# Time attention with one mixed block of scores a step, layer-norm roots by ScalarE, and both additions of weights on POOL

## The chip, the cores and the metric

One core of one Trainium2 chip. The metric is the device time of the whole kernel in microseconds (us). Executions repeat within 0.3% for all but one of the kernels below; that one has a section of its own. Kernels sent together ran on the same chip beside runs of the kernel before.

## The reference

The input x has 2 x 256 x 128 x 128 float32 elements (batch, time T, bands FB, channels C). One layer, three residual parts:

```python
xt = _ln(x, ln_t_w, ln_t_b).transpose(0, 2, 1, 3)
x = x + _mha(xt, t_wi, t_bi, t_wo, t_bo, 4, causal_mask(256)).transpose(0, 2, 1, 3)   # over time
xf = _ln(x, ln_f_w, ln_f_b)
x = x + _mha(xf, f_wi, f_bi, f_wo, f_bo, 4, band_mask(128, 16))                       # over bands
xn = _ln(x, ln_n_w, ln_n_b)
x = x + (gelu(xn @ w1.T + b1) @ w2.T + b2)                                            # feed-forward
# _ln: (x - mean) * rsqrt(var + 1e-5);  _mha: 4 heads of 32 channels, softmax
```

All bias vectors of the inputs are zero. This matters for one experiment.

## The kernel before

Everything stays in float32. Work goes in groups of 512 rows (four tiles of 128). For time attention a group is two sequences of 256 steps, so the causal scores of a sequence have three blocks of 128x128: first keys with both halves of the queries (256 columns), second keys with the second half (128 columns). There are 128 such groups, one in each step of a software pipeline. All instructions of an engine run in program order. The code is shortened:

```python
def root(self):                                    # layer norm, on POOL: (var + EPS) ** -0.5
    gpsimd.tensor_scalar(self.rstd, self.mv[:, :, 1], EPS, None, ALU.add)
    gpsimd.tensor_tensor(self.rstd, self.rstd, path.k.mhalf, ALU.pow)
def normalize(self):                               # VectorE, four tiles: xh
    for i in range(NT):
        vector.tensor_scalar(self.xh[:, i, :], self.src()[:, i, :], self.mv[:, i, 0:1], self.rstd[:, i : i + 1],
                             ALU.subtract, ALU.mult)
def bias(self):                                    # POOL: residual + folded bias row -> res
    self.path.gpsimd.tensor_tensor(self.dst(), self.src(), orow_of_this_attention, ALU.add)
def divide(self):                                  # VectorE: softmax division with one Newton step
    vector.tensor_tensor(by_rows(t), by_tile(self.rp), by_tile(self.r0), ALU.mult)
    vector.tensor_tensor(by_rows(u), by_tile(self.op), by_tile(self.r0), ALU.mult)
    vector.scalar_tensor_tensor(self.oT, t, 2.0, u, ALU.subtract, ALU.mult)
# ... (cut)
class OverTime(Attention):
    def scores(self, s):                           # sequence s: four heads = four row tiles of 32
        for h in range(H):
            path.tensor.matmul(self.sp[h][:, 0:2*P], self.kT[r, a:a+P], self.qT[r, a:a+2*P], ...)
        for h in range(H):
            path.tensor.matmul(self.sp[h][:, 2*P:3*P], self.kT[r, a+P:a+2*P], self.qT[r, a+P:a+2*P], ...)
    # exp on ScalarE (128x384 a head), two causal masks of 128x512 a sequence on POOL,
    # one addition of weights on POOL (sequence 0), one on VectorE (sequence 1)
# ... (cut)
def bank(self, shape, name):                       # PSUM: eight buffers of one tag
    return self.ps.tile(shape, F32, name=name, tag="ps")
```

On TensorE the projections, sums and outputs work on four column tiles (128x32 weights). The scores work on four row tiles (32x128 weights), in two blocks a step, one for each sequence.

## Time and profile before

| | before |
|---|---|
| median | 2786.06 us (2785.55 to 2786.35, 3 runs) |
| 128 time groups | 46 to about 1040 us, 7.63 us a step on TensorE |
| bands and feed-forward | the remaining 1745 us, not meant to change |
| engines, 200 to 962 us, of 762 | PE 762, VectorE 671, ScalarE 614, POOL 702 |

PE is TensorE's matmuls, PEld its weight loads, DVE is VectorE, ACT is ScalarE. A timeline line gives the start, the duration, engine, operation, output and inputs, shapes and how many in a row. In brackets stands the idle time ahead of it and what ended that time. The tiles: qp, kp and vp are the projections, sp the scores, rp the sums of the softmax, op the weighted values, yp the output product; r, t, u and oT belong to the division; stats and mv are the statistics of the layer norm, rstd its root, xh the normalized rows, z their transpose; res is the residual, first with the bias row (POOL), then with yp added (VectorE). For "steps" I take the differences between the starts of rp, once a step on TensorE. The lines themselves are in the prediction.

### The profile page before, as it was taken

What the parts mean: (1) busy time and instruction counts of PE and PEld (TensorE: products, weight loads), DVE (VectorE), ACT (ScalarE), POOL (GpSimd) and SP (SyncE); (2) the same over time, 40 slices, a digit from 0 to 9 for tenths busy, and PEclk for the clock granted to TensorE, in tenths of its full rate; (3) what the DMA queues carried; (4) which work ended last, traced back from release to release, by engine and by line L of the source; (5) the groups of instructions that cost most, each with busy time, mean ns of one, the idle gap of its engine ahead of it and who ended that gap; (6) DMA issues with size and microseconds to landing.
All of it is one profiled execution on the core that took longest, in us unless ns stands there. A gap on an engine that the chain in (4) does not pass through costs nothing.

```text
span 2785.2 us, 103938 instructions
## 1 busy us (share of the span) xinstructions
PE 2730.3 (98%) x42534; PEld 1867.5 (67%) x42534; DVE 2221.5 (80%) x6446; ACT 1800.0 (65%) x3328; POOL 2079.3 (75%) x2569
## 2 busy tenths in 40 slices
PE   4999999999999989999999999999999999999998
PEld 3666666666666657776777777777777767767776
DVE  5888888888888898778678687687786786876874
ACT  2888888878888866646556556456466465574563
POOL 3899999999999997667676676676676666766762
PEclk9999999999999999999999999999999999999999
DMA  5555555555555554544544544535545445444333
GB/s 121 135 147 137 137 141 143 146 132 146 139 142 135 146 134 117 129 117 102 140 105 111 132 106 123 130 100 127 127 99 137 104 108 130 113 117 114 91 92 85
DMA packets 471301, 343.70 MB, mean 123 GB/s; under 512 B 43296, under 2 KB 405152, under 8 KB 470816
## 3 DMA queue, kind: packets, MB, share of 16 engines
q1 hardware_dynamic: 469568, 335.92, 47.5%
q8 instruction: 337, 5.52, 0.9%
q14 instruction: 148, 1.21, 0.2%
q10 hardware_dynamic: 1248, 1.05, 0.1%
HBM read 169.03 MB, written 167.77 MB: 121 GB/s over the span
## 4 chain that ended last, share of the span: by engine, by line
PE 93%; DVE 3%; DMA 2%; POOL 1%; issue 0%; SPq 0%; ACT 0%; DVEq 0%; POOLq 0%
PE zp L848 17%; PE hp L848 16%; PE sp L848 12%; PE op L848 10%; PE qp L848 8%; PE rp L848 8%; PE vp L848 8%; PE yp L848 7%; PE kp L848 7%; POOL pt L848 1%; DMA x<-in_x 1%; DVE xh L848 1%; DMA xnT<-turned 1%; DVE oT L848 0%; POOL rstd L848 0%; DVE stats L848 0%
## 5 line engine op out<-in xcount | busy, mean ns | idle before, releaser
L848 ACT ACTIVATE hT<-hp,b 128x512 f32<-128x512 f32 x512 | 348.7, 687 | 546.0 <-PE hp L848 536.1
L848 POOL TENSOR_SCALAR_AFFINE_SELECT pf<-pf 128x512 f32<-128x512 f32 x768 | 541.5, 720 | 173.5 <-ACT pf L848 147.1
L848 PEld LDWEIGHTS zp<-w2T_sb,hT 128*128 128x128 f32 x4096 | 476.4, 192 | 56.1 <-issue 54.0
L848 DVE TENSOR_SCALAR xh<-x,mv,rstd 128x128 f32<-128x128 f32 x1536 | 509.2, 392 | 0.4 <-POOL rstd L848 0.4
L848 PE MATMUL zp<-w2T_sb,hT 128*128 128x128 f32 x4096 | 479.8, 275 | 0.1
L848 PE MATMUL hp<-xnT,w1f 128*128 128x512 f32 x1024 | 469.2, 596 | 3.6 <-DMA xnT<-turned 3.4
L848 POOL TENSOR_TENSOR rstd<-rstd,mhalf 128x4 f32<-128x4 f32 x384 | 441.3, 1149 | 32.0
L848 ACT ACTIVATE pt<-sp 128x384 f32<-128x384 f32 x1024 | 419.5, 497 | 58.8 <-PE sp L848 58.8
L848 PE MATMUL sp<-qT,kT 32*128 32x128 f32 (+1 forms) x8192 | 389.5, 315 | 0.8 <-ACT kT L848 0.8
L848 POOL TENSOR_SCALAR_AFFINE_SELECT pt<-pt 128x512 f32<-128x512 f32 x512 | 322.7, 651 | 79.0 <-ACT pt L848 79.0
L848 PEld LDWEIGHTS sp<-qT,kT 32*128 32x128 f32 x8192 | 310.9, 185 | 79.7 <-issue 31.1
L848 POOL TENSOR_SCALAR rstd<-mv 128x4 f32<-128x4 f32 x384 | 89.2, 232 | 365.5 <-DVE mv L848 365.1
L848 DVE BATCH_NORM_STATS2 stats<-x 128x6 f32<-128x128 f32 x1536 | 329.0, 274 | 7.6 <-DMA x<-in_x 7.6
L848 ACT ACTIVATE pf<-sp 128x512 f32<-128x512 f32 x512 | 264.3, 603 | 58.8 <-PE sp L848 52.4
L848 PEld LDWEIGHTS hp<-xnT,w1f 128*128 128x128 f32 x1024 | 182.2, 190 | 178.9 <-issue 109.6
L848 PE MATMUL qp<-xnT,wf 128*32 128x512 f32 (+1 forms) x1856 | 273.1, 600 | 26.2 <-DVE xh L848 26.2
L848 PEld LDWEIGHTS yp<-wn,oT 128*32 128x32 f32 (+1 forms) x7808 | 240.8, 111 | 84.0 <-issue 63.2
L848 PEld LDWEIGHTS vp<-wf,xnT 128*32 128x32 f32 (+1 forms) x7424 | 241.1, 113 | 70.4 <-issue 60.2
L848 DVE STREAM_TRANSPOSE z<-xh 128x512 f32<-128x512 f32 x384 | 273.2, 711 | 18.9 <-DMA turned<-z 5.8
L848 PE MATMUL yp<-wn,oT 128*32 128x128 f32 (+1 forms) x7808 | 277.9, 273 | 0.3 <-DVE t L848 0.3
L848 DVE TENSOR_TENSOR res<-zp,res 128x512 f32<-128x512 f32 x128 | 87.6, 685 | 234.8 <-PE zp L848 234.7
L848 PE MATMUL vp<-wf,xnT 128*32 128x128 f32 (+1 forms) x7424 | 273.5, 273 | 0.5 <-DVE t L848 0.5
(90 smaller groups left out, 4072.8 us busy)
## 6 DMA issues: line engine op xcount, KB each, us to landing
turned<-z SPq DMA_DIRECT2D x1536, 64.0 KB, 2.2
xnT<-turned SPq DMA_DIRECT2D x384, 256.0 KB, 2.8
x<-in_x SPq DMA_DIRECT2D x128, 256.0 KB, 4.8
x<-res SPq DMA_DIRECT2D x256, 128.0 KB, 3.4
x<-x SPq DMA_DIRECT2D x128, 256.0 KB, 4.1
out<-res SPq DMA_DIRECT2D x256, 128.0 KB, 2.4
w1T_sb<-in_w1T ACTq DMA_DIRECT2D x1, 256.0 KB, 3.9
w2T_sb<-in_w2T ACTq DMA_DIRECT2D x1, 256.0 KB, 4.2
```

The lines of the kernel that those rows point to most:

```text
L848: return self.tc.keep_in_program_order(emit(*args, **kwargs))
```

## The change

Each switch to row tiles costs TensorE time (about 0.36 us in this trace, worked out in the prediction), so the change makes one block of scores a step out of two. The short second-key scores of group n and the long first-key scores of group n+1 are issued together, with the heads interleaved so that the four row tiles have equal work. That moves the pipeline of the time groups one step earlier. To make room on POOL for both additions, the roots go to ScalarE as Exp(-0.5 Ln(var + eps)), followed by one Newton step of three tiny VectorE instructions. Each PSUM bank becomes a tag of its own, so that banks can be placed by hand. The diff, shortened:

```diff
+    def root_by_scalar(self):
+        var = self.mv[:, :, 1]
+        path.scalar.activation(ln, var, AF.Ln, bias=path.eps)
+        path.scalar.activation(y, ln, AF.Exp, scale=-0.5)
+        vector.scalar_tensor_tensor(t, var, EPS, y, ALU.add, ALU.mult)
+        vector.scalar_tensor_tensor(t, t, -0.5, y, ALU.mult, ALU.mult)
+        vector.scalar_tensor_tensor(self.rstd, t, 1.5, y, ALU.add, ALU.mult)
 ... (cut)
-    def last_sum(self):
-        self.add(self.path.vector, 1)
+    def mask(self, blk):                  # one mask of 128x1024 for two of 128x512
+    def add(self, s):
+        self.path.gpsimd.tensor_tensor(self.p1[:, s, :, 1], self.p1[:, s, :, 0], self.p0[:, s, :, P : 2 * P], ALU.add)
+def time_scores(old, new):
+    for h, second, s in (
+        (0, 1, 0), (1, 0, 0), (2, 0, 0), (3, 1, 0), (0, 1, 1), (3, 1, 1), (0, 0, 0), (3, 0, 0),
+        (1, 0, 1), (2, 0, 1), (0, 0, 1), (3, 0, 1), (1, 1, 0), (2, 1, 0), (1, 1, 1), (2, 1, 1),
+    ):
+        if second and old is not None:
+            old.second_scores(h, s)
+        if not second and new is not None:
+            new.first_scores(h, s)
 ... (cut: order of the step)
+            if old is not None or new is not None:
+                time_scores(old, new)
+                Attention.place = dict(rp=b["b0"], op=b["b3"], yp=b["a1"], qp=b["a2"], kp=b["b1"], vp=b["b2"])
+                old.mask_second()
+                old.add(0)
+                new.mask_first()
+                old.add(1)
-            do_at(n + 4, OverTime, "root")
+            do_at(n + 5, OverTime, "root_by_scalar")
 ... (cut)
-        return self.ps.tile(shape, F32, name=name, tag="ps")
+            i, self.next_bank = self.next_bank, (self.next_bank + 1) % 8
+        return self.ps.tile(shape, F32, name=name, tag=f"ps{i}")
```

More of the change, by code (lines that the diff above doesn't have):

```diff
@@ L468, in root @@
         gpsimd.tensor_tensor(self.rstd, self.rstd, path.k.mhalf, ALU.pow)
+    def root_by_scalar(self):
+        path, vector = self.path, self.path.vector
+        var = self.mv[:, :, 1]
+        ln = path.small.tile([P, NT], F32, name="lnv")
+        path.scalar.activation(ln, var, AF.Ln, bias=path.eps)
+        y = path.small.tile([P, NT], F32, name="y")
+        path.scalar.activation(y, ln, AF.Exp, scale=-0.5)
+        t = path.small.tile([P, NT], F32, name="vy")
+        vector.scalar_tensor_tensor(t, var, EPS, y, ALU.add, ALU.mult)
+        vector.scalar_tensor_tensor(t, t, -0.5, y, ALU.mult, ALU.mult)
+        self.rstd = path.small.tile([P, NT], F32, name="rstd", bufs=16)
+        vector.scalar_tensor_tensor(self.rstd, t, 1.5, y, ALU.add, ALU.mult)
     def normalize(self):
@@ L512, in second_mask @@
         pass
-    def last_sum(self):
-        pass
     def queries_keys(self):
@@ L549 @@
     which = None
+    place = {}
     def bias(self):
@@ L558, in queries_keys @@
         wf = path.k.wf[self.which]
-        self.qp = path.bank([P, NT * P], "qp")
+        self.qp = path.bank([P, NT * P], "qp", self.place.get("qp"))
         product(path, self.qp, wf[:, 0:P], self.xnT)
-        self.kp = path.bank([P, NT * P], "kp")
+        self.kp = path.bank([P, NT * P], "kp", self.place.get("kp"))
         product(path, self.kp, wf[:, P : 2 * P], self.xnT)
@@ L577, in values @@
         wv = path.k.wf[self.which][:, 2 * P : 3 * P]
-        self.vp = path.bank([P, NT, P], "vp")
+        self.vp = path.bank([P, NT, P], "vp", self.place.get("vp"))
         for i in range(NT):
@@ L583, in take_values @@
         path = self.path
-        self.v = path.work.tile([P, NT, P], F32, name="v")
+        self.v = path.work.tile([P, NT, P], F32, name="v", bufs=4)
         path.scalar.copy(self.v, self.vp)
@@ L617, in output @@
         path = self.path
-        self.yp = path.bank([P, NT, P], "yp")
+        self.yp = path.bank([P, NT, P], "yp", self.place.get("yp"))
         for i in range(NT):
@@ L646, with first_tiles @@
     which = 0
-    W = 3 * P
-    def scores(self, s):
+    early, late = (1, 2), (0, 3)
+    def first_tiles(self):
         path = self.path
-        W, a = self.W, 2 * s * P
-        self.sp = [path.bank([P, W], "sp") for h in range(H)]
-        for h in range(H):
-            r = rows_of(h)
-            path.tensor.matmul(
-                self.sp[h][:, 0 : 2 * P], self.kT[r, a : a + P], self.qT[r, a : a + 2 * P], start=True, stop=True
-            )
-        for h in range(H):
-            r = rows_of(h)
-            path.tensor.matmul(
-                self.sp[h][:, 2 * P : W], self.kT[r, a + P : a + 2 * P], self.qT[r, a + P : a + 2 * P],
-                start=True, stop=True,
-            )
@@ L665, in weights @@
-    def weights(self, s):
-        path = self.path
-        for h in range(H):
-            path.scalar.activation(self.p[:, s, h, 0 : self.W], self.sp[h], AF.Exp)
-    def mask(self, s):
-        path = self.path
-        for n in (2, 0):
-            blk = self.block(s, n)
-            path.gpsimd.affine_select(
-                out=blk, in_=blk, compare_op=ALU.is_ge, fill=path.zero, base=0,
-                pattern=[[0, H], [1, P]], channel_multiplier=-1,
-            )
-    def block(self, s, n):
-        return self.p[:, s, :, n * P : (n + 1) * P]
@@ L682, in add @@
-    def add(self, engine, s):
-        engine.tensor_tensor(self.block(s, 3), self.block(s, 1), self.block(s, 2), ALU.add)
-    def first_half(self):
-        self.p = self.path.work.tile([P, 2, H, self.W + P], F32, name="pt", tag="p", bufs=2)
-        self.scores(0)
-    def first_function(self):
-        self.weights(0)
-    def first_mask(self):
-        self.mask(0)
-        self.add(self.path.gpsimd, 0)
-    def second_half(self):
-        self.scores(1)
-    def second_function(self):
-        self.weights(1)
@@ L702, in second_mask @@
-    def second_mask(self):
-        self.mask(1)
-    def last_sum(self):
-        self.add(self.path.vector, 1)
-    def weigh_one(self, op, s):
-        path, p, v, W = self.path, self.p, self.v, self.W
-        for h in range(H):
-            r = rows_of(h)
-            path.tensor.matmul(op[r, s, :], v[:, 2 * s, r], p[:, s, h, 0 : 2 * P], start=True, stop=False)
-        for h in range(H):
-            r = rows_of(h)
-            path.tensor.matmul(
-                op[r, s, P : 2 * P], v[:, 2 * s + 1, r], p[:, s, h, 2 * P : W], start=False, stop=True
-            )
@@ L719, in weigh @@
-    def weigh(self):
-        path = self.path
-        op = path.bank([P, 2, 2 * P], "op")
-        rp = path.bank([P, 2, 2 * P], "rp")
-        self.weigh_one(op, 0)
-        sums = self.p.rearrange("p s h (n q) -> p s h n q", q=P)[:, :, :, 0:4:3, :]
-        for h in range(H):
-            path.tensor.matmul(rp[rows_of(h), :, :], path.k.ones[:, 0:D], sums[:, :, h], start=True, stop=True)
-        self.weigh_one(op, 1)
-        self.op = op.rearrange("p s q -> p (s q)")
-        self.rp = rp.rearrange("p s q -> p (s q)")
+        self.p0 = path.work.tile([P, 2, H, 2 * P], F32, name="p0", tag="p", bufs=3)
@@ new lines, in first_tiles, with second_tiles, first_scores @@
+        self.s0 = {h: path.bank([P, 2, 2 * P], "sp", path.banks[f"a{h}"]) for h in range(H)}
+    def second_tiles(self):
+        path = self.path
+        self.p1 = path.work.tile([P, 2, H, 2, P], F32, name="p1", tag="h", bufs=2)
+        self.s1 = {h: path.bank([P, 2, P], "sp", path.banks[f"b{h}"]) for h in range(H)}
+    def first_scores(self, h, s):
+        r, a = rows_of(h), 2 * s * P
+        self.path.tensor.matmul(
+            self.s0[h][:, s], self.kT[r, a : a + P], self.qT[r, a : a + 2 * P], start=True, stop=True
+        )
@@ new lines, in second_scores, with first_weights, second_weights @@
+    def second_scores(self, h, s):
+        r, a = rows_of(h), (2 * s + 1) * P
+        self.path.tensor.matmul(
+            self.s1[h][:, s], self.kT[r, a : a + P], self.qT[r, a : a + P], start=True, stop=True
+        )
+    def first_weights(self, heads):
+        for h in heads:
+            self.path.scalar.activation(self.p0[:, :, h], self.s0[h], AF.Exp)
+    def second_weights(self, heads):
+        for h in heads:
+            self.path.scalar.activation(self.p1[:, :, h, 0], self.s1[h], AF.Exp)
@@ new lines, in mask, with mask_first, mask_second @@
+    def mask(self, blk):
+        path = self.path
+        path.gpsimd.affine_select(
+            out=blk, in_=blk, compare_op=ALU.is_ge, fill=path.zero, base=0,
+            pattern=[[0, 2], [0, H], [1, P]], channel_multiplier=-1,
+        )
+    def mask_first(self):
+        self.mask(self.p0[:, :, :, 0:P])
+    def mask_second(self):
+        self.mask(self.p1[:, :, :, 0])
+    def add(self, s):
+        self.path.gpsimd.tensor_tensor(self.p1[:, s, :, 1], self.p1[:, s, :, 0], self.p0[:, s, :, P : 2 * P], ALU.add)
@@ new lines, in weigh @@
+    def weigh(self):
+        path, v = self.path, self.v
+        rp = path.bank([P, 2, 2, P], "rp", self.place.get("rp"))
+        for n in range(2):
+            for h in range(H):
+                w = self.p1[:, :, h, 1] if n else self.p0[:, :, h, 0:P]
+                path.tensor.matmul(rp[rows_of(h), :, n], path.k.ones[:, 0:D], w, start=True, stop=True)
+        op = path.bank([P, 2, 2 * P], "op", self.place.get("op"))
+        for s in range(2):
+            for h in range(H):
+                r = rows_of(h)
+                path.tensor.matmul(op[r, s, :], v[:, 2 * s, r], self.p0[:, s, h], start=True, stop=False)
+            for h in range(H):
+                r = rows_of(h)
+                path.tensor.matmul(
+                    op[r, s, P : 2 * P], v[:, 2 * s + 1, r], self.p1[:, s, h, 0], start=False, stop=True
+                )
+        self.op = op.rearrange("p s q -> p (s q)")
+        self.rp = rp.rearrange("p s n q -> p (s n q)")
@@ new lines, in time_scores @@
+def time_scores(old, new):
+    if new is not None:
+        new.first_tiles()
+    if old is not None:
+        old.second_tiles()
+    for h, second, s in (
[6 more added lines that the diff above has]
+            new.first_scores(h, s)
@@ L767, in first_half @@
     def first_half(self):
-        self.p = self.path.work.tile([P, H, NT, P], F32, name="pf", tag="p", bufs=2)
+        self.p = self.path.work.tile([P, H, NT, P], F32, name="pf", tag="p", bufs=3)
         self.scores(range(H))
@@ L810, in first_half @@
         self.hp = {}
-        self.hT = self.path.work.tile([P, self.path.k.NI, NT * P], F32, name="hT")
+        self.hT = self.path.work.tile([P, self.path.k.NI, NT * P], F32, name="hT", tag="h", bufs=2)
         self.hidden((0, 1))
@@ L858, in __init__ @@
         self.small = ctx.enter_context(tc.tile_pool(name="small", bufs=6))
-        self.ps = ctx.enter_context(tc.tile_pool(name="ps", bufs=8, space=PSUM))
+        self.ps = ctx.enter_context(tc.tile_pool(name="ps", bufs=1, space=PSUM))
+        self.next_bank = 0
+        self.banks = dict(zip(("a1", "a2", "b0", "b3", "a0", "a3", "b1", "b2"), range(8)))
         self.tensor, self.vector = InOrder(tc, tc.nc.tensor), InOrder(tc, tc.nc.vector)
@@ L864, in __init__ @@
         once = ctx.enter_context(tc.tile_pool(name="once", bufs=1))
+        self.eps = once.tile([P, 1], F32, name="eps")
+        tc.nc.vector.memset(self.eps, EPS)
         self.band = once.tile([P, P], F32, name="band")
@@ L872, in __init__, with bank @@
             )
-    def bank(self, shape, name):
-        return self.ps.tile(shape, F32, name=name, tag="ps")
+    def bank(self, shape, name, i=None):
+        if i is None:
+            i, self.next_bank = self.next_bank, (self.next_bank + 1) % 8
+        return self.ps.tile(shape, F32, name=name, tag=f"ps{i}")
     @staticmethod
@@ L978, in run @@
             turn = feeds[2] and bands[1]
+            old, new = (groups[i] if at(i, OverTime) else None for i in (n, n + 1))
             self.by_columns = at(n - 1, Attention)
             do(n + 11, "load")
-            do_at(n + 4, OverTime, "statistics")
             if bands[2] and feeds[1]:
@@ L985, in run @@
             do(n, "first_half", "first_function", "first_mask")
+            if old is not None or new is not None:
+                time_scores(old, new)
+                b = self.banks
+                Attention.place = dict(rp=b["b0"], op=b["b3"], yp=b["a1"], qp=b["a2"], kp=b["b1"], vp=b["b2"])
+            else:
+                Attention.place = {}
+            if old is not None:
+                old.second_weights(old.late)
+            if new is not None:
+                new.first_weights(new.early)
+            if old is not None:
+                old.second_weights(old.early)
+                old.mask_second()
+                old.add(0)
             if turn:
                 do(n, "second_half", "second_function")
-            do_at(n + 2, Attention, "fetch")
+            do_at(n + 3, OverTime, "fetch")
+            do_at(n + 2, OverBands, "fetch")
             do_at(n + 1, FeedForward, "fetch")
             do_at(n + 2, FeedForward, "normalize", "turn")
-            do_at(n + 3, Attention, "normalize", "turn")
-            do_at(n + 4, OverTime, "root")
+            do_at(n + 3, OverBands, "normalize", "turn")
+            do_at(n + 4, OverTime, "normalize", "turn")
+            do_at(n + 5, OverTime, "statistics")
             if bands[2]:
@@ L996, in run @@
             do(n - 1, "invert_exactly" if turn else "invert")
-            if bands[2] or turn:
+            if new is not None:
+                new.first_weights(new.late)
+                new.mask_first()
+            if old is not None:
+                old.add(1)
+            if bands[2] or turn or old is not None:
                 do(n - 2, "output", "finish")
@@ L1008, in run @@
                 if not turn:
-                    do_at(n + A, OverBands, "statistics", "root")
-            do(n + 1, "queries_keys", "take_query", "take_key")
-            if not bands[2] and not turn:
-                do(n - 2, "output", "finish")
-            do(n + 1, "values", "take_values")
-            do(n, "last_sum")
+                    do_at(n + A, OverBands, "statistics")
+                    if not at(n, OverTime):
+                        do_at(n + A, OverBands, "root")
+            do_at(n + 2, OverTime, "queries_keys", "take_query", "take_key")
+            do_at(n + 1, OverBands, "queries_keys", "take_query", "take_key")
+            do_at(n + 5, OverTime, "root_by_scalar")
+            if at(n - 1, OverTime):
+                do_at(n + A - 1, OverBands, "root_by_scalar")
+            if not bands[2] and not turn and old is None:
+                do(n - 2, "output", "finish")
+            do_at(n + 2, OverTime, "values", "take_values")
+            do_at(n + 1, OverBands, "values", "take_values")
+            if old is not None or new is not None:
+                b = self.banks
+                self.banks = dict(
+                    a1=b["a1"], a2=b["a2"], b0=b["a0"], b3=b["a3"], a0=b["b0"], a3=b["b1"], b1=b["b3"], b2=b["b2"]
+                )
 def bounded_path(tc, k, x, out):
```

## The prediction

> **What bounds the kernel now.** I read the page's busy shares first, then the busy time by stretch, then the timeline of one step on TensorE, and last the groups and the timeline of VectorE and POOL for what they wait on each other.
>
> ```profile
> PE 2730.3 (98%) x42534; PEld 1867.5 (67%) x42534; DVE 2221.5 (80%) x6446; ACT 1800.0 (65%) x3328; POOL 2079.3 (75%) x2569
> ```
>
> PE covers the whole span. The 128 time-attention groups run from 46 us to about 1040 us, one group a step; only they change. The stretches (PE, PEld, DVE, ACT, POOL busy) show two regimes there:
>
> ```profile
> 200.00:962.00 762.00, 762.00 (x15190) 480.33 (x15190) 671.09 (x1801) 613.56 (x1300) 702.09 (x800) 1.00 0.55 141
> 962.00:1034.00 72.00, 64.41 (x1268) 39.96 (x1264) 70.80 (x178) 50.77 (x108) 70.76 (x80) 1.00 0.48 123
> ```
>
> For 762 us PE never idles. In the last 72 us (the last eight steps, which also normalize the first band groups) DVE and POOL are 98% busy and PE idles 7.6 us. One step on PE:
>
> ```profile
> 507.23 0.94 PE L848 MATMUL sp<-qT,kT 32*128 32x256 f32 x16
> 508.10 1.06 PE L848 MATMUL qp<-xnT,wf 128*32 128x512 f32 x8
> 508.98 1.04 PE L848 MATMUL kp<-xnT,wf 128*32 128x512 f32 x8
> 509.84 1.06 PE L848 MATMUL yp<-wn,oT 128*32 128x128 f32 x32
> 510.71 1.06 PE L848 MATMUL vp<-wf,xnT 128*32 128x128 f32 x32
> 511.70 0.94 PE L848 MATMUL sp<-qT,kT 32*128 32x256 f32 x16
> 512.56 0.86 PE L848 MATMUL op<-pt,v 128*32 128x256 f32 x16
> 513.24 1.04 PE L848 MATMUL rp<-pt,ones 128*32 128x512 f32 x8
> 514.09 0.83 PE L848 MATMUL op<-pt,v 128*32 128x256 f32 x16
> 514.86 0.94 PE L848 MATMUL sp<-qT,kT 32*128 32x256 f32 x16
> ```
>
> Read the differences of starts, since the ends are modelled: the step is 514.86 - 507.23 = 7.63 us. Products of 512 columns on four column tiles take 0.86 (kp, yp, rp). A block of scores streams 384 columns a row tile, so 384/512 x 0.86 = 0.645 us, but lasts 0.87: 0.22 over. The product ahead of a block is longer too: vp 0.99 against yp's 0.87 (0.12), the second op 0.77 against 0.645. Each block of row tiles so costs about 0.22 + 0.12 + 0.02 = **0.355 us** beside its streaming, twice a step.
>
> **What the Trainium skill says.** "TensorEngine Tiling (Array Packing)", Key Properties: a change of tiling mode drains TensorE. The trace agrees; above is its price here. "TensorE: Matmul & The Clock Gate", LDWEIGHTS: a load costs by its columns, whatever its rows; this agrees with 185 ns for 32x128 weights against 110 for 128x32, and with the first pass of a block being late. "GPSIMD Engine Reference", Key points: it shares SBUF interfaces with VectorE and contends with instructions in a 2-port mode or with two SBUF inputs. The trace agrees, strongly:
>
> ```profile
> 501.89 0.69 DVE L848 SCALAR_TENSOR_TENSOR oT<-t,u 128x512 f32<-128x512 f32 x1
> 994.29 1.28 POOL L848 TENSOR_TENSOR pt<-pt 128x512 f32<-128x512 f32 x1
> 994.36 1.77 DVE L848 SCALAR_TENSOR_TENSOR oT<-t,u 128x512 f32<-128x512 f32 x1
> 506.21 1.39 DVE L848 TENSOR_SCALAR xh<-x,mv,rstd 128x128 f32<-128x128 f32 x4
> 998.50 1.71 POOL L848 TENSOR_TENSOR res<-x,orow 128x512 f32<-128x512 f32 x1
> 999.00 3.05 DVE L848 TENSOR_SCALAR xh<-x,mv,rstd 128x128 f32<-128x128 f32 x4
> ```
>
> oT alone is 0.69 us; begun inside POOL's addition it ends 0.55 us after the addition does. The four xh take 1.1 to 1.4 us, or 3.05 when POOL has work one after another: each then waits out one whole POOL instruction. Masks (0.63) hold DVE as additions do; the tiny pow (1.04) does not: xh runs beside it at 0.34. Stats, the transpose and what reads PSUM (t, u, res) are never held. "ScalarE: Activation LUTs", Table sets: ln and exp share a set, so roots on ACT should need no table load; the Ln and Exp of the reciprocal already alternate here without one.
>
> **The change, part by part.**
> *PE.* The first-key-block scores of group n+1 and the second-key-block scores of group n are issued as one block: still 768 columns a row tile, 1.29 us. The heads' order gives row tiles 0 and 3 the short ones first and 1 and 2 the long ones, so all finish together if tiles run independently; today's records show h0 to h3 starting 7 ns apart, so I assume it. One of two blocks' 0.355 us goes: step 7.63 - 0.355 = **7.27 us**, the floor. Over 120 full steps: -42.6 us.
> *ACT.* Eight exps of 384 become four of 512 and four of 256: starts lie 0.37 apart now, 0.48 for 512 and, by the slope, 0.265 for 256: 2.98 us both ways. Added: Ln and Exp of 128x4, about 0.45 us. From 613.56/100 = 6.14 to 6.6 us a step. Fits. kT ends about 0.85 us after kp does (as in the bands) and vp lasts 0.98, so the scores should not wait for it.
> *POOL.* Removed: the root, 0.23 + 1.15 a step. Two masks of 1024 for four of 512: 2 x 1.08 (estimate from 292 ns at 128 and 630 at 512) for 2.52. Added: one addition, 1.29. Left: 2.16 + 3 x 1.26 = 5.95 of work, against 7.03 busy with waits.
> *DVE.* Minus the addition (1.06), plus three 128x4 instructions (0.15 to 0.2 each, like small ones here): 6.71 - 1.06 + 0.5 = 6.15.
> Each engine fits 7.27 alone. **Together DVE and POOL hardly do.** All of POOL's 5.95 us now hold the interface; the pow, which didn't, is gone. And DVE's contending instructions now stand in a row: oT, three small root instructions (two SBUF inputs), four xh.
> By hand, from the start of the scores: all second exps end 2.9, so POOL runs first mask 2.96 to 4.03, addition to 5.25, second mask to 6.3, addition to 7.57, bias after it. DVE's res waits for yp until 4.85, then t, u; oT is ready at 6.8, waits for the second addition and ends 8.1; bias then holds until 9.25, the root's three wait for it, and xh starts at 9.75, that is 2.5 in the next step. Two xh pass, then the mask comes at 2.96, and the last two wait until 4.05 and 5.3. res comes at 7.1 to 7.8, while PE's next block wants its bank (yp's) at 7.27. PE waits about 0.6, and 0.3 more for op's bank behind u. That delay lets xh pass freely in the following step, and the next good one fails again: 7.27 and about 8.15 in turn, mean 7.7. Were xh 0.35 us earlier, all would fit and 7.27 would hold. My timings are no better than that, so I take the mean of 7.27 and 7.7, **7.5**, as expected: 120 x (7.63 - 7.5) = -16 us.
> *Last eight steps.* Now 8.15, 8.47, 9.71, 9.70, 9.55, 8.32, 8.33, 8.32 between sums on PE. Without the roots POOL has 5.95 + 1.27 (band bias) = 7.2, DVE 6.15 + 1.5 (band statistics and roots), plus waits for each other: some 8.2 each, -5 us.
> *Fill.* One more step of software pipeline: 0 to +2 us. Bands and feed-forward keep their order on the engines; their buffers stay sufficient.
> Sum: 2786 - 16 - 5 = 2765.
>
> **Rivals.** (1) *The floor holds*: 7.27 everywhere; -42.6, about -8 at the tail: 2735. For it: PE is at 100% with other engines under 92%, and the author placed every bank so that it is freed in time. Against it: the interface. (2) *The interface becomes the bound*: 7.7 or a bit more: 2790. For it: the hand timetable; the last eight steps of before, where PE idles with DVE and POOL saturated. (3) *The mixed block doesn't run level* (a row tile waits in order behind a longer one): up to 0.21 us, one 128-column pair, of the gain gone, 25 us: about 2760 without contention. Nothing in the trace has mixed lengths. (4) *kT or v late on ACT* behind the small roots: under 0.1 us a step.
>
> **Range and chances.** Over 2% faster needs below 2730, beyond even rival 1: 5%. Over 2% slower needs a step above 8.1 us: 4%. Predicted 2764, from 2735 (rival 1) to 2803 (rival 2 with a longer tail or a ragged block).
>
> **What would show it.** Steps on PE between starts of rp: 7.27 flat (rival 1), or alternating 7.27 and 8+ (rival 2). The scores' block should last 1.29 + 0.22 with one gap of 0.12 ahead; more is rival 3. Under rival 2 the waits show scores on PE released by DVE (res or u), and means of xh and oT above 392 and 839 ns. I am wrong if small root instructions are not held by POOL, for then xh is early enough; or if the new block loses more than it saves.

## The result and the profile after

The changed kernel takes **2835.03 us** (median of 4 runs, 2831.26 to 2838.56) beside 2785.81 us of the kernel before in the same rounds. The ratio is 1.0177 (95% interval 1.0159 to 1.0194). Here and below, a ratio is the mean time of one kernel's fast runs over that of the other's fast runs of the same rounds, so not quite the ratio of the medians. The change is slower, by less than 2%. The prediction had it within 2% too, but faster (2764), and the time lies outside its range of 2735 to 2803.

The page's busy line of the changed kernel:

```profile
PE 2746.9 (97%) x43522; PEld 1925.3 (68%) x43522; DVE 2344.7 (83%) x6727; ACT 1848.4 (65%) x3600; POOL 1964.1 (69%) x2169
```

Its busy time by stretch (PE, PEld, DVE, ACT, POOL, then the mean granted clock, DMA share and GB/s), the steady time steps and the last eight, which start later here than before (the first at 1001.7 us):

```profile
200.00:962.00 762.00, 739.76 (x15440) 515.81 (x15432) 741.68 (x1933) 625.66 (x1447) 598.51 (x484) 1.00 0.54 136
1001.70:1078.25 76.55, 63.94 (x1224) 44.28 (x1222) 75.21 (x188) 48.70 (x116) 58.04 (x48) 0.91 0.45 108
```

VectorE went from 671 to 742 of 762 us, 97%, although on paper it lost work. POOL fell from 702 to 599. PE, which never idled in the first stretch before, is idle for 22 us by this view (ends of matmuls are modelled, so the view tells less of the waiting than the steps do). The chain that ended last says the same:

```profile
PE 64%; DVE 27%; DMA 5%; issue 1%; SPq 1%; ACT 1%; DVEq 0%; POOL 0%
```

Before, PE had 93% of it and VectorE 3%. The steps on PE alternate: 7.29, 8.40, 7.29, 8.40. Their mean over steps 20 to 110 is 7.84 against 7.63 before. What makes a long step, from the timeline (rp starts at 511.23 and again at 519.61, 8.38 us; the last line on VectorE already belongs to the next round):

```profile
508.93 1.28 POOL L862 TENSOR_TENSOR p<-p,p 128x512 f32<-128x512 f32 x1
509.25 1.51 DVE L862 SCALAR_TENSOR_TENSOR oT<-t,u 128x512 f32<-128x512 f32 x1
509.71 1.59 PE L862 MATMUL sp<-qT,kT 32*128 32x128 f32 x32
...
510.16 1.73 POOL L862 TENSOR_TENSOR res<-x,orow 128x512 f32<-128x512 f32 x1
...
510.68 1.23 DVE L862 SCALAR_TENSOR_TENSOR vy<-mv,y 128x4 f32<-128x4 f32 x1
...
511.23 1.07 PE L862 MATMUL rp<-p,ones 128*32 128x256 f32 x16
...
512.34 3.02 DVE L862 TENSOR_SCALAR xh<-x,mv,rstd 128x128 f32<-128x128 f32 x4
...
512.82 1.09 POOL L862 TENSOR_SCALAR_AFFINE_SELECT p<-p 128x1024 f32<-128x1024 f32 x1 [0.93 <-ACT p L862]
...
514.00 1.28 POOL L862 TENSOR_TENSOR p<-p,p 128x512 f32<-128x512 f32 x1
...
517.00 0.48 PE L862 MATMUL sp<-qT,kT 32*128 32x128 f32 x2
517.06 0.66 DVE L862 TENSOR_TENSOR res<-yp,res 128x512 f32<-128x512 f32 x1
...
517.86 1.82 PE L862 MATMUL sp<-qT,kT 32*128 32x256 f32 x30 [0.38 <-DVE res L862]
...
518.94 0.69 DVE L862 SCALAR_TENSOR_TENSOR oT<-t,u 128x512 f32<-128x512 f32 x1
...
519.61 1.07 PE L862 MATMUL rp<-p,ones 128*32 128x256 f32 x16
```

Read it from the top. oT, 0.69 us by itself, waits for POOL's addition and takes 1.51. POOL's bias waits for oT and takes 1.73. The first tiny root instruction (four elements a partition, 0.15 us by itself) waits for the bias and takes 1.23. The other two need its result and run free behind it (0.17 and 0.16). So xh starts only at 512.34, 0.45 us after the bias has ended. The first mask comes half a microsecond later, and the third and fourth xh are held by it and by the next addition: four xh take 3.02 us, where they take 1.1 when free. Then transpose, statistics and res follow, and res ends at 517.71. PE wanted the bank that res reads at 517.0. Two matmuls of the block run; the other thirty start at 517.86, over 0.8 us late. Later parts of the block wait for t and u as well. PE thereby loses about 1.1 us (8.40 - 7.29) in a long step. The delay gives VectorE air: in the next step oT takes 0.69 and nothing is held, and then it begins anew.

The waits of the stretch 200 to 962 us (total, times, longest) name two things at that place:

```profile
PEld sp L862 <- ACT y L862: 30.0, 48, 2.8
...
PE sp L862 <- DVE res L862: 22.2, 48, 2.7
```

The first line looks as if ScalarE's root y, late because its Ln waits for VectorE's statistics, held the block too. Experiment 5 was made on that reading, and the reading was wrong.

Where the whole difference lies, from the starts of rp in the two profiled executions (+51.6 us):

| part | before | after | difference |
|---|---|---|---|
| until the first sums | 54.4 | 59.1 | +4.7 |
| steps 1 to 3 | 24.1 | 28.1 | +3.9 |
| steps 4 to 119 | 884.7 | 914.5 | +29.8 |
| last eight steps | 70.5 | 76.6 | +6.0 |
| to the first sums of the bands | 6.2 | 8.7 | +2.5 |
| bands and feed-forward | 1679.7 | 1684.2 | +4.6 |

Steps 4 to 119 of this execution contain one disturbance, two steps of 11.8 and 9.0.

A part of this is the clock. The granted clock of the changed kernel is 0.50 in five short stretches of the time part, 68.0 to 74.8, 934.9 to 941.8, 1020.3 to 1027.1, 1057.8 to 1061.2 and 1074.9 to 1081.7 us, and 1.00 elsewhere from 47 to 2832 us; in the kernel before it is 1.00 from 45 to 2723 us. Each of the five begins in a wait of PE for VectorE, of 2.7 to 4.9 us, or (the fourth) 1.0 us after one of 1.8. The block behind the wait at 935 us:

```profile
935.35 2.94 PE L862 MATMUL sp<-qT,kT 32*128 32x256 f32 x30 [2.69 <-DVE res L862]
```

From its start to that of rp it takes 2.86 us, where a whole block takes 1.52 at the full clock. So the disturbance, a part of steps 1 to 3 and a part of the last eight steps are work at half the clock. In the last eight steps PE is busy for 11.4 us of such stretches; half of that, 5.7 us, is an estimate of what they cost at most. The alternation of 7.29 and 8.40 itself is at 1.00. No experiment here tests what lowers the clock.

### The profile page after: what moved, and what is told of

It is laid out like the page before. It is cut to its first block, busy times and chain, and to the rows that moved or that the text cites. A ratio compares the mean times of both kernels' runs of the same rounds, so it can differ in the third digit from the quotient of the medians.

```text
span 2836.8 us, 106281 instructions
## 1 busy us (share of the span) xinstructions
PE 2746.9 (97%) x43522; PEld 1925.3 (68%) x43522; DVE 2344.7 (83%) x6727; ACT 1848.4 (65%) x3600; POOL 1964.1 (69%) x2169
## 3 DMA queue, kind: packets, MB, share of 16 engines
q14 instruction: 150, 1.23, 0.2%
## 4 chain that ended last, share of the span: by engine, by line
PE 64%; DVE 27%; DMA 5%; issue 1%; SPq 1%; ACT 1%; DVEq 0%; POOL 0%
PE zp L862 16%; PE hp L862 15%; DVE xh L862 8%; PE sp L862 6%; PE rp L862 5%; PE op L862 4%; PE vp L862 4%; PE qp L862 4%; PE kp L862 4%; PE yp L862 4%; DVE oT L862 3%; DVE stats L862 3%; DVE z L862 3%; DVE vy L862 2%; DVE res L862 2%; DMA turned<-z 2%
## 5 line engine op out<-in xcount | busy, mean ns | idle before, releaser
L862 DVE TENSOR_SCALAR xh<-x,mv,rstd 128x128 f32<-128x128 f32 x1536 | 595.0, 450 | 4.6
L862 POOL TENSOR_SCALAR_AFFINE_SELECT p<-p 128x1024 f32<-128x1024 f32 x256 | 288.2, 1126 | 246.1 <-ACT p L862 246.1
L862 PE MATMUL sp<-qT,kT 32*128 32x128 f32 (+1 forms) x8192 | 414.1, 316 | 41.8 <-DVE res L862 33.1
L862 ACT ACTIVATE p<-sp 128x512 f32<-128x512 f32 (+1 forms) x1024 | 417.3, 500 | 45.2 <-PE sp L862 38.9
L862 PEld LDWEIGHTS sp<-qT,kT 32*128 32x128 f32 x8192 | 350.8, 187 | 103.2 <-ACT kT L862 44.0
L862 POOL TENSOR_TENSOR p<-p,p 128x512 f32<-128x512 f32 x256 | 327.4, 1279 | 10.7
L862 POOL TENSOR_SCALAR rstd<-mv 128x4 f32<-128x4 f32 x248 | 56.5, 228 | 357.6 <-DVE mv L862 357.3
L862 PE MATMUL qp<-xnT,wf 128*32 128x512 f32 (+1 forms) x1850 | 267.1, 593 | 28.5 <-DMA xnT<-turned 26.4
L862 ACT ACTIVATE qT<-qp,bq 128x512 f32<-128x512 f32 x256 | 176.1, 688 | 166.3 <-PE qp L862 166.3
L862 PE MATMUL yp<-wn,oT 128*32 128x128 f32 (+1 forms) x7808 | 271.0, 273 | 0.0
```

What stands on the lines that cost most here:

```text
L862: return self.tc.keep_in_program_order(emit(*args, **kwargs))
```

## The experiments

Theory A: POOL's bias holds the first of the refinement's three small instructions, the other two depend on it, together they push xh into POOL's masks, and that delay closes a loop through res to TensorE. Main rival (D): VectorE simply has too much to do.

| | edit against the changed kernel | median us | ratio to before | steps, us |
|---|---|---|---|---|
| 1 | block alone: roots on POOL, second addition on VectorE | 2758 or 2904 | see below | 7.29 or 8.54 |
| 2 | only the roots back on POOL | 3024.45 | 1.0859 | 9.53 (mean) |
| 3 | only the second addition back on VectorE | 2774.03 | 0.9958 | 7.35 (mean) |
| 4 | no refinement | 2753.75 | 0.9889 | 7.29 flat |
| 5 | Ln and Exp behind the copy of v | 2862.95 | 1.0269 | 8.12 (mean) |
| 6 | three unheld instructions for the refinement | 2754.34 | 0.9881 | 7.29, few longer |
| 7 | refinement, but a tiny bias | 2758.41 | 0.9901 | 7.29 flat |
| 8 | block alone, pushed once | 2762.93 | 0.9913 | 7.29, two longer after the push |
| 9 | kernel before with PSUM tags of the change | 2824.51 | 1.0133 | 7.91 (mean) |
| 10 | one of the three small instructions | 2752.86 | 0.9878 | 7.29 flat |
| 11 | number 1 again | 2757 or 2906 | see below | 8.54 in the profile |

All were correct, number 7 only because of its inputs (see there).

### 1. The block alone

```diff
-            if old is not None:
-                old.add(1)
+            do_at(n + 5, OverTime, "root")          # POOL, behind the mask
 ...
             do(n - 1, "divide")
+            if old is not None:
+                old.add(1)                          # on VectorE
-            do_at(n + 5, OverTime, "root_by_scalar")
```

> The new block of scores alone: roots back on POOL (between second mask and bias), the addition for the second half back on DVE after oT. Theory A (DVE and POOL hold each other's SBUF interface; the pow leaves it free and the addition holds it 0.55 us on DVE instead of 1.26 on POOL): every step at the floor of 7.29 us, about 2760 us in all. Rival B (the new block with its banks is what costs, by ragged row tiles or late banks): steps stay near the 7.84 mean of the change, 2820 to 2840.

Four runs: 2759.09, 2758.0, 2906.6 and 2901.3 us, on the same chip, at the same granted clock (0.996 to 0.999). The profiled run is a fast one, with steps of 7.29 almost throughout. So the mixed block brings the floor by itself, without roots on ScalarE. But the kernel has a second, slow rhythm. Experiments 8 and 11 look at it.

### 2. Roots alone back on POOL

```diff
                 new.mask_first()
+            do_at(n + 5, OverTime, "root")
             if old is not None:
                 old.add(1)
 ...
-            do_at(n + 5, OverTime, "root_by_scalar")
```

> Only the roots back on POOL, both additions stay there. POOL then has 5.95 + 1.38 = 7.3 us of work a step, as much as the floor. Theory A: about 7.6 us a step (7.4 to 7.8), since POOL has no slack for a wait but the pow lets oT pass: some 2805 us. Rival C (the roots on ACT and DVE are the whole harm): 7.29 flat, 2760.

It took 3024.45 us, ratio 1.0859 (1.084 to 1.0877), much slower than expected. POOL is busy 608 of 762 us, so it isn't full. Its timeline:

```profile
600.16 0.23 POOL L862 TENSOR_SCALAR rstd<-mv 128x4 f32<-128x4 f32 x1 [1.95 <-DVE mv L862]
600.47 1.04 POOL L862 TENSOR_TENSOR rstd<-rstd,mhalf 128x4 f32<-128x4 f32 x1
601.49 1.27 POOL L862 TENSOR_TENSOR p<-p,p 128x512 f32<-128x512 f32 x1
602.71 1.74 POOL L862 TENSOR_TENSOR res<-x,orow 128x512 f32<-128x512 f32 x1
604.41 1.09 POOL L862 TENSOR_SCALAR_AFFINE_SELECT p<-p 128x1024 f32<-128x1024 f32 x1
```

The root stands in POOL's queue ahead of the second addition and waits 1.95 us for VectorE's statistics. These come behind four xh, and in the same step the four xh take 4.76 us because they are held by the POOL instructions that follow the root. POOL waits for VectorE and VectorE for POOL, in one ring of 9.7 us. Neither is full by its own work (VectorE shows 756 of 762 us busy, but that counts the time in which it is held); the ring is the bound. (The mean granted clock is 0.96 in that stretch, because of short parts at 0.50.) Rival C falls as well.

### 3. Second addition on VectorE

```diff
-        self.path.gpsimd.tensor_tensor(self.p1[:, s, :, 1], ...)
+        (self.path.vector if s else self.path.gpsimd).tensor_tensor(self.p1[:, s, :, 1], ...)
 ...                                   # and add(1) stands behind "divide"
```

> Only the second addition back on DVE, after oT; roots stay on ACT and DVE. POOL has 4.7 us of work, DVE 6.8. Theory A: POOL's gap grows by 1.26 us, so roots and xh pass in it: 7.29 to 7.45 us a step, 2760 to 2785 in all. Rival D (DVE simply has too much work, 97% busy in the change): DVE gets 0.55 us more a step and the mean rises above 7.84, over 2840.

It took 2774.03 us, ratio 0.9958 (0.9941 to 0.9974), with steps of 7.29 to 7.39. VectorE has one instruction more and the kernel is 61 us faster than the changed one. Rival D falls: what counts is what POOL has to do at that place, not VectorE's amount of work.

### 4. No refinement

```diff
-        path.scalar.activation(y, ln, AF.Exp, scale=-0.5)
-        vector.scalar_tensor_tensor(t, var, EPS, y, ALU.add, ALU.mult)
-        vector.scalar_tensor_tensor(t, t, -0.5, y, ALU.mult, ALU.mult)
-        vector.scalar_tensor_tensor(self.rstd, t, 1.5, y, ALU.add, ALU.mult)
+        path.scalar.activation(self.rstd, ln, AF.Exp, scale=-0.5)
```

> The change, but the root is Exp's output itself: the three small DVE instructions that refine it are gone (less exact, still close). Theory A: xh waits for the bias once instead of the small ones and then starts 0.5 us earlier, all four before the next mask: 7.29 flat, about 2765 us. If the small instructions are not what makes xh late: alternating steps stay, 2815 to 2835.

It took 2753.75 us, ratio 0.9889 (0.9872 to 0.9905): every step of 20 to 110 is 7.29. It is faster than both kernels, at the price of the Newton step (the result passes the comparison with the reference). VectorE and POOL in a step:

```profile
604.50 1.61 DVE L857 SCALAR_TENSOR_TENSOR oT<-t,u 128x512 f32<-128x512 f32 x1
...
605.52 1.73 POOL L857 TENSOR_TENSOR res<-x,orow 128x512 f32<-128x512 f32 x1
...
606.03 2.07 DVE L857 TENSOR_SCALAR xh<-x,mv,rstd 128x128 f32<-128x128 f32 x4
...
608.10 1.09 POOL L857 TENSOR_SCALAR_AFFINE_SELECT p<-p 128x1024 f32<-128x1024 f32 x1 [0.85 <-ACT p L857]
```

oT and the first xh are held as before, but the other three xh pass in the gap of 0.85 us between the bias and the mask, and end at 608.10, as the mask starts.

### 5. Roots behind the copy of v

```diff
-            do_at(n + 5, OverTime, "root_by_scalar")
             do_at(n + 2, OverTime, "values", "take_values")
+            do_at(n + 5, OverTime, "root_by_scalar")
```

> The changed kernel with one move: ScalarE's Ln and Exp of the roots stand behind its copy of v instead of ahead of it. The waits of the changed kernel name 18.7 us of Ln waiting for late statistics in 48 of the long steps, about 0.39 us each, with v behind it. Theory A (this queueing is what makes the long step 8.40 instead of the predicted 8.15): steps still alternate, 7.29 and about 8.1, mean about 7.70, 13 to 20 us less: 2815 to 2822. Rival B (v is late, but the step is set by the held VectorE chain, and nothing is regained, or the refinement now waits for the Exp instead): steps as before, 2830 to 2845.

It took 2862.95 us, ratio 1.0269 (1.0252 to 1.0286), 28 us slower than the changed kernel. Both theories missed. The queue behind Ln isn't what lengthens the long step. The waits view had split one gap in two lines: in the records of the changed kernel res ends at 517.713 and y at 517.709, 4 ns apart, and a separate wait on VectorE, released by res, stands in TensorE's queue directly ahead of the third weight load of the block. The gap belongs to res; y was merely the last ScalarE event. That this order is worse still (7.29, 8.64, 9.6 and 10.4 in patterns of some three steps) shows how much the rhythm depends on order. The steps of 10.4, and those of 7.9 to 9.0 behind some of the long ones, lie in stretches at a granted clock of 0.50; those of 8.64 and 9.6 don't. For these I have no simple sum.

### 6. Three unheld instructions in the refinement's place

```diff
+        path.scalar.activation(self.rstd, ln, AF.Exp, scale=-0.5)
+        for i in range(3):
+            spare = path.small.tile([P, 2], F32, name="spare")
+            vector.bn_aggr(spare, self.stats[:, i, :])
```

> The kernel without the refinement (2753.75 measured), plus three extra variance aggregations of 0.15 us on VectorE in the refinement's place, into a spare tile: the same number of instructions and about the same time, but of a kind that ran beside POOL's work unheld so far. Theory A (the refinement costs through being held behind POOL's bias): still 7.29 flat, 2752 to 2760. Rival C (any half microsecond more on VectorE between oT and xh tips the loop): steps alternate again, 2790 to 2835.

It took 2754.34 us, ratio 0.9881 (0.9865 to 0.9898). The mean step is 7.33, with nearly all at 7.29.

```profile
605.50 0.30 DVE L860 BATCH_NORM_AGGREGATE spare<-stats 128x2 f32<-128x6 f32 x3
605.73 1.84 DVE L860 TENSOR_SCALAR xh<-x,mv,rstd 128x128 f32<-128x128 f32 x4
```

Three instructions of 0.15 us that aren't held cost nothing. They end at 605.81 while the bias still runs (to 606.71), and the first xh is held by the bias to 606.80 in any case. The refinement can't hide so: it only starts when the bias has ended. The three overlap to 0.30 us, against 0.5 of the refinement, so the dose is a little smaller.

### 7. The refinement with a tiny bias

```diff
+    def bias(self):                       # 128x4 elements instead of 128x512
+        self.path.gpsimd.tensor_tensor(self.dst()[:, :, 0:1], self.src()[:, :, 0:1], orow[:, 0:1] ..., ALU.add)
+    def finish(self):
+        self.path.vector.tensor_tensor(self.dst(), self.yp, self.src(), ALU.add)
```

> The changed kernel with the refinement kept, but POOL's bias of a time group reduced from 128x512 to 128x4 elements; the last addition on VectorE takes x itself. The result is wrong on purpose (the time attention's bias row is missing). Theory A (POOL's 1.7 us bias between oT and xh is what holds the refinement and the first xh): steps 7.29 flat, 2750 to 2762. Rival C (the refinement is too much for VectorE by itself): mean step above 7.6, over 2790.

It took 2758.41 us, ratio 0.9901 (0.9884 to 0.9917), flat 7.29. The kernel leaves out the bias row on purpose. It still passed, because the biases of these inputs are zero; it is no version to keep. With the bias gone the same three instructions run at 0.15 to 0.16 us and the four xh unheld:

```profile
606.22 0.15 DVE L873 SCALAR_TENSOR_TENSOR vy<-mv,y 128x4 f32<-128x4 f32 x1
...
606.80 1.12 DVE L873 TENSOR_SCALAR xh<-x,mv,rstd 128x128 f32<-128x128 f32 x4
```

Experiments 4, 6 and 7 together show theory A: remove the held instructions, or replace them by unheld ones, or remove what holds them, and the steps are at the floor. Number 7 also takes most of a 1.26 us instruction a step from POOL; 4 and 6 take nothing from it.

### 8 and 11. The second rhythm of the block alone

```diff
                 new.mask_first()
+                if n == 30:
+                    new.mask(self.idle)       # two masks of 128x1024 on a spare tile, once
+                    new.mask(self.idle)
```

> The block-alone kernel (roots on POOL, second addition on VectorE), whose four runs lay at 2758 twice and at 2901 and 2907 twice, with one disturbance: in step 30 POOL does two extra masks of 128x1024 on a spare tile, about 2.2 us, once. Theory F (its loop of POOL and VectorE has two rhythms, 7.29 and about 8.5 a step, and what falls into the long one stays there): steps of 7.29 up to step 30 and about 8.5 from there to the end of the time groups, all runs at 2870 to 2900. Rival G (the loop heals after a push, and the two slow runs had another cause): one or a few long steps after step 30, then 7.29 again, 2758 to 2765 in most runs.

All four runs lie at 2762 to 2765. The profile shows steps of 12.3 and 8.9 after the push, then 7.29 again. Such a push heals; theory F in that form is refuted.

> The block-alone kernel once more, unchanged, because two of its first four runs lay at 2758 and two at 2901 to 2907, and a push in step 30 healed within two steps. If it has a second rhythm, some of these six runs lie at about 2900 again and a profile may show it: steps of 8.5 instead of 7.29. If the two slow runs were an accident of that chip, all lie at 2755 to 2765.

The unchanged repeat gave 2904.98, 2911.81, 2906.88, 2754.07, 2756.84, 2903.03 and 2758.26 us. By the rule of 1.5% the long runs count as "slow", but there is no lower clock (0.996 to 0.998 in all), so this is no state of the chip. The ratio over the fast runs is 0.9885 (0.9867 to 0.9903). The profiled execution was a slow one. Its steps are 8.54 from the third on to the end, so it was set at the start:

```profile
606.18 1.27 POOL L862 TENSOR_TENSOR res<-x,orow 128x512 f32<-128x512 f32 x1
...
606.56 1.44 DVE L862 SCALAR_TENSOR_TENSOR oT<-t,u 128x512 f32<-128x512 f32 x1
...
607.92 0.68 DVE L862 TENSOR_TENSOR p<-p,p 128x512 f32<-128x512 f32 x1
...
608.74 0.64 PE L862 MATMUL rp<-p,ones 128*32 128x256 f32 x8 [0.88 <-DVE p L862]
```

Here oT comes 0.4 us after POOL's bias has begun and is held by it. VectorE's addition stands behind oT, and TensorE's sums wait for that addition. In the fast profile of the same program oT slips in while POOL does its small root, runs free (0.69), and the pow waits instead (1.48). The same program has two stable orders of who waits for whom. What decides between them in the first steps stays open.

### 9. The tags of the PSUM banks by themselves

```diff
-        self.ps = ctx.enter_context(tc.tile_pool(name="ps", bufs=8, space=PSUM))    # kernel before
+        self.ps = ctx.enter_context(tc.tile_pool(name="ps", bufs=1, space=PSUM))
-        return self.ps.tile(shape, F32, name=name, tag="ps")
+        i, self.next_bank = self.next_bank, (self.next_bank + 1) % 8
+        return self.ps.tile(shape, F32, name=name, tag=f"ps{i}")
```

> The kernel before with one thing of the change only: each PSUM bank is its own one-buffer tag, taken in the same rotation, instead of eight buffers of one tag. The program's work and order stay. In the changed kernels the bands and feed-forward take 2.1 to 4.6 us longer between their first and last sums, and the last row tile of a band's scores starts 0.21 us after the first instead of level. Theory A (the tags bring separate waits on TensorE's queue, which make the block ragged): the stretch of bands and feed-forward goes from 1679.7 to about 1682, and the ragged start is seen; the whole kernel 0 to +10 us, for time's two blocks a step would then be ragged too. Rival B (the tags change nothing; it is the time stage's state or buffers that the bands inherit): 1679.7 within 0.7, level starts, whole kernel within 2 us of before.

Bands and feed-forward go from 1679.7 to 1681.85 us, as theory A of this run expected. The fourth row tile of the bands' score blocks starts 0.02 us after the first in the kernel before; here it does so in some blocks and starts 0.14 to 0.21 us later in others, with a separate wait in TensorE's queue ahead of its weight load. So some 2 of the 4.6 us that the changed kernel loses there come with the tags. The whole kernel went to 2824.51 us (ratio 1.0133, 1.0117 to 1.0148), which I had not expected. The time steps have pairs of 8.15 and 8.96 among those of 7.63, with one wait that the kernel before doesn't list:

```profile
PEld yp L848 <- DVE u L848: 71.9, 97, 2.0
```

The output product waits for a bank that u still reads. It looks as if the eight-buffer tag had handed out other banks than a fixed rotation does; I didn't follow that up. In the changed kernel the banks of the time steps are placed by hand, and in experiment 4 no such wait is left (7.29 flat), so this loss doesn't carry over to its time steps.

### 10. One of the three small instructions

```diff
+        path.scalar.activation(self.rstd, ln, AF.Exp, scale=-0.5)
+        vector.scalar_tensor_tensor(spare, var, EPS, self.rstd, ALU.add, ALU.mult)
```

> The kernel without the refinement (2753.75, all steps 7.29), plus one of its three small instructions with two SBUF inputs in its place, into a spare tile, as a measure of the dose: 0.2 us between the end of POOL's bias and the first xh. Without the refinement the fourth xh ends at the very moment at which POOL's first mask starts (608.10 against 608.10), so one instruction more should leave the fourth xh to wait for that mask, 1.1 us. Theory A (the loop has some slack behind that, since half a microsecond of unheld work was absorbed): 7.29 flat or with few long steps, 2754 to 2770. Rival H (any held xh tips it): 7.29 and 8 or more in turn, 2790 to 2835.

It took 2752.86 us, ratio 0.9878 (0.9863 to 0.9893), at 7.29 but for three of the steps 20 to 110 (7.34 to 7.44).

```profile
604.81 1.77 DVE L859 SCALAR_TENSOR_TENSOR oT<-t,u 128x512 f32<-128x512 f32 x1
606.50 0.15 DVE L859 SCALAR_TENSOR_TENSOR spare<-mv,rstd 128x4 f32<-128x4 f32 x1
```

As expected the fourth xh is held by the mask (1.17 us), and that is absorbed: rival H falls. But the run isn't the measure of the dose that it was meant to be. In 92 of 100 steps the small instruction isn't held at all (0.15 us), because POOL's bias now starts just ahead of oT (604.76), holds oT instead, and is over at 606.03. So the loop has slack for one held xh. In the changed kernel two of them are held, by the mask and by the addition behind it. What one held small instruction costs stays unmeasured.

## Why the prediction was wrong

- **The floor was right.** 7.27 predicted (its three terms give 0.36 and not 0.355 a block), 7.29 measured in experiments 4, 7 and 10. The block takes 1.52 us from its start to that of rp, against 1.29 + 0.22. Row tiles with works of different length run level, so rival 3 didn't occur.
- **The holds were right.** oT waits for the second addition, bias for oT, the root's first instruction for the bias, xh for mask and addition, res comes late, PE waits for it. Each step of the hand timetable is in the records, and the signs that the prediction named for rival 2 came: xh has a mean of 450 ns (above 392), oT of 1009 (above 839). Its margin was about right too: it said that 7.27 would hold were xh 0.35 us earlier; in experiment 10 xh starts 0.76 us ahead of the first mask instead of 0.48, and 7.29 holds. One reading was loose: in its example of 3.05 us only two of the four xh are held (1.30 and 1.32), not each.
- **The step that failed: "I take the mean of 7.27 and 7.7, 7.5".** The two were cases of which one holds, not ends of a scale. The timetable itself said rival 2, and the measured steps alternate as it said. With 7.5, the steady steps were booked as a gain of 16 us; they lost 29.8.
- **The long step was mis-sized.** 8.15 predicted, 8.40 measured. PE's wait for res is over 0.8 instead of 0.6. From the block's start, the hand timetable has the mask at 2.96 to 4.03 and the fourth xh's end at 5.3. The records have 3.11 to 4.20 and 5.65 (512.82, 513.91 and 515.36 less 509.71). Small differences, such as the later start of the mask and the 0.08 us between mask and addition, add up in a ring where every instruction waits for the one before. The mean is 7.84 instead of 7.7.
- **The tail was wrong in sign.** -5 predicted, +6.0 measured. In those eight steps VectorE is busy 75.2 of 76.5 us, now also with held small instructions, and PE waits up to 4.9 us for it at one block; up to 5.7 us are work at half the clock (the estimate above). Without the refinement the tail takes 69.6 (experiment 4).
- **Fill and bands were too small.** Fill: 0 to +2 predicted, +8.6 measured up to step 3, a part of it in the stretch at half the clock from 68.0 us. Experiment 4 has +3.3 there, which stays with any version that has one pipeline step more. Bands: 0 predicted, +4.6 measured; some 2 come with the tags (experiment 9).
- **Why the range missed.** Its upper end, 2803, was rival 2 with a little tail. Rival 2 at its own sizes gave 2790. The longer steps (116 x 0.18, about 21; 914.5/116 is 7.88, with the disturbance), the fill (8), the tail (11), the way to the bands (2.5) and the bands (4.6) make the other 47 us. They all erred in one direction, and the range treated them as nearly nothing.
- **Rival 4 was right to be small.** Exp and Ln aren't on the path, although a line of the waits suggests it (experiment 5). "ScalarE: Activation LUTs", Table sets, on which the prediction rests here, held: both profiles have 32 table loads.

The gain the change is meant to bring exists: the floor of 7.29 is worth about 39 us in steps 4 to 119 (884.7 less 845.3). It was turned into a wait by three instructions of 0.16 us, of which the first is held and the other two depend on it.

## What to carry to other kernels

When two engines share an interface and each runs in order, don't add up their work: write down the order of their instructions and see who waits for whom around the ring, and believe that timetable rather than averaging it with the case in which it doesn't happen. A tiny instruction costs the whole instruction that holds it, so put such ones where the other engine is idle, make them of a kind that isn't held (here statistics, 0.27 us, aggregation, 0.15, the 32x32 transpose, 0.71, and additions with one input in PSUM, 0.68, kept their times beside POOL's masks and additions), or leave them out. A kernel can have two stable rhythms at one clock: look at every run's time, not at the median.

## What the Trainium skill lacked or had wrong

- "GPSIMD Engine Reference", Key points, says that POOL shares its SBUF interfaces with VectorE and contends with instructions in a 2-port mode or with two SBUF inputs. The runs agree, in both directions: a 128x4 instruction of 0.15 us took 1.23 us beside the bias, and the bias 1.73 instead of 1.26 us behind a running oT. No page has how long after the end of the POOL instruction the held one ends: here 20 ns for the 128x4 instruction, 80 ns for xh, 550 ns for oT.
- No page makes an exception for a POOL instruction on a tiny tile. Here the pow of 128x4 takes 1.04 us, and xh that starts inside it keeps its 0.34 us (27 of 27 in the time part of the kernel before); inside masks and additions it is held.
- No page tells that such sharing can give a program two rhythms: 2754 to 2759 us or 2901 to 2912 us for the same kernel at a clock of 0.996 to 0.999.
- "TensorEngine Tiling (Array Packing)", Key Properties, says that tiles operate independently. That held for row tiles with work of mixed length (1.52 us for a block estimated at 1.51). The page doesn't say that waits in TensorE's queue between them stagger their starts: 0.02 us became up to 0.21 us in the bands' blocks with more PSUM tags, in a run that took 2.2 us longer over the bands.
